# A graph kernel on one core: another order of a pair's products in layer 0, one buffer for x1, banks chosen by hand

## The chip, the core and the metric

The kernel runs on one core of a Trainium2 chip. A core has five engines that run side by side, each through its own list of instructions in order: TensorE (PE in the profile: matmuls; PEld are its weight loads), VectorE (DVE), ScalarE (ACT), GpSimd (POOL) and SyncE (SP), which here issues all the DMAs. An instruction that needs what another engine makes waits on a semaphore, and everything behind it on its own engine waits too. The metric is the time of one execution on the device in microseconds (us), median of several runs.

## The reference

Two layers of a graph network in float32, on 64 graphs of 256 nodes with 256 features, all with one 256 x 256 adjacency:

```python
# layer 0, with G = adj * adj
h = relu(layernorm(x))
h = relu(G @ (h @ W1))          # W1: 256 x 512
h = relu(G @ (h @ W2))          # W2: 512 x 1024
x = x + G @ (h @ W3)            # W3: 1024 x 256
# layer 1, with U the eigenvectors of the normed Laplacian of adj
h = relu(layernorm(x))
h = relu((U.T @ h) @ W1 + b1)   # W1: 256 x 128
x = x + U @ (h @ W2 + b2)       # W2: 128 x 256
```

So the kernel has two jobs that do not depend on each other until layer 1: the eigenvectors of one 256 x 256 matrix (a long chain of small steps, mostly on VectorE), and the matmuls of layer 0 (TensorE).

## The kernel before, in words

**Layer 0** (class `Layers`) goes over 32 pairs of graphs. For pair q the products on TensorE are `first` (G h0, 8 matmuls of 256 columns, copied to y1 by ScalarE), `widened` (times W1, 8 matmuls of 512, relu to s1), `spread_out` (times G, 16 of 256, copied to y2), `third` (times W2, 32 of 512, relu to s2), `fourth` (times W3, 32 of 256, copied to p3) and `last` (G p3, 4 of 512; VectorE adds x and writes x1). Then `norm1` normalizes x1 on ScalarE and GpSimd, `turn_rows` transposes it (8 of 128), `for_layer1` multiplies by layer 1's W1 (8 of 128) and gives hw. x1 and hw go to memory by a DMA, but those of the last two pairs (`KEPT = 2`) stay on the chip.

A float32 matmul of n columns shows as two records in the profile. Every product goes to a PSUM bank of 128 x 512; layer 0 has four, handed out by a pool in turn, and a bank can be taken again when ScalarE or VectorE has read it.

**The order of the work** is written down by `products` (the line of TensorE's work and the ScalarE operations behind it) and `rows` (loads and norms). The order within pair q before is: third(q), turn_rows(q-1), the first half of fourth(q), for_layer1(q-1), first(q+1), the second half of fourth(q), widened and spread_out of q+1, last(q). `rows` begins pair q+1 (load x, norm to h0) and then does norm1 of pair q-1.

**The eigenvectors** (class `Eigen`) share the engines with it. `Pace` is a planner that runs while the program is built: it keeps a clock for each engine with estimated durations, and before each operation of the eigenvector chain it fills the engines with operations from the two streams that fit before that operation is due. It may cut a matmul at a multiple of 128 columns. So the lists of TensorE and ScalarE hold layer 0 and the eigenvector chain interleaved in a fixed order; a wrong estimate becomes a wait. SP has no clock in the plan: a DMA counts as landed 4 us after its data is ready.

At the end of the chain, a flag says whether a rare repair is needed (`mend`): all engines load the flag and branch on it. `pace.go_on(FLAG_US)` puts 3.5 us of TensorE work between the flag's product and the branch. Behind the branch `layer1` runs: a third stream (`layer1_of`) fetches hw and x1 of a pair (`fetch`, two DMAs), multiplies hw by U (`to_vectors`), by U again (`from_vectors`) and by W2 (`finish`), 4 matmuls of 256 each, and writes the output. What is left of layer 0 goes on beside it.

Of the kernel before, what the change touches and what calls it, by code (L numbers as in the profile page):

```python
# [27 lines left out]
N = 256  # L28
P = 128
H = 2  # L30
PAIRS = 32
KEPT = 2
# [48 lines left out]
class Op:  # L81
# [4 lines left out]
    def __init__(self, part, call, args, kwargs):  # L86
# [18 lines left out]
        elif self.engine == "ACT":  # L105
            pointers = any(isinstance(kwargs.get(k), bass.AP) for k in ("scale", "bias"))
            self.busy = 0.13 + n / 1400 + 0.12 * pointers + 0.19 * sums
            self.until = self.busy + 0.12
        elif self.engine == "DVE":
            each = 6.3 if self.name == "reciprocal" else 2.0 if self.name == "tensor_tensor_scan" else 1.0  # L110
            pointers = self.name == "scalar_tensor_tensor" or any(a.shape[1:] == [1] for a in ins[1:])
            self.busy = 0.065 + 0.06 * pointers + each * n / 960 + 0.08 * sums
            self.until = self.busy + 0.125
        elif self.engine == "POOL":
            power = OP.pow in args
            self.busy = 0.2 + (0.14 * n + 0.15 if power else 2 * n / 960)
            self.until = self.busy + 0.1
        else:
            self.busy, self.until = 0.1, 4.0
# [160 lines left out]
class Eigen:  # L280


    def __init__(self, tc, ctx, ap, gt2, pace):
# [5 lines left out]
        self.adj = pool.tile([P, H, N], F32, name="adj")  # L289
        dma(out=self.adj, in_=ap["adj"].rearrange("(h p) n -> p h n", p=P))  # L290
        mats = [pool.tile([P, H, N], F32, name=c) for c in ("ident", "lower", "upinc", "sub")]
        self.mats = mats
        self.ident, self.lower, self.upinc, self.sub = mats
        self.load_matrices(0, 1)
# [9 lines left out]
        self.mp = ctx.enter_context(tc.tile_pool(name="eig_mat", bufs=1))  # L304
# [1465 lines left out]
class Layers:  # L1770


    def __init__(self, tc, ctx, ap, gt2, u, ut):
# [3 lines left out]
        self.kept = ctx.enter_context(tc.tile_pool(name="kept", bufs=KEPT))  # L1777
        dram = ctx.enter_context(tc.tile_pool(name="dram", bufs=1, space=bass.MemoryType.DRAM))
        self.x1, self.hw = {}, {}
        self.x, self.h0, self.y1, self.y2, self.s2, self.p3, self.h1, self.new = ({} for _ in range(8))  # L1780
        self.begun, self.through, self.rows_of = set(), set(), {}
        self.due = False
        self.spilled = {
            q: dram.tile([P, H * 2 * N], F32, name=f"x1_{q}") for q in range(PAIRS - KEPT)
        }
        self.spilled_hw = {
            q: dram.tile([P, H * 2 * P], F32, name=f"hw_{q}") for q in range(PAIRS - KEPT)
        }
# [20 lines left out]
    def load(self, q):  # L1809
        self.x[q] = x = self.io.tile([P, H, 2, N], F32, tag="x", name="x")  # L1810
# [5 lines left out]
    def open(self, ctx):  # L1816

        self.io = ctx.enter_context(self.tc.tile_pool(name="l0_io", bufs=2))
        self.wp = ctx.enter_context(self.tc.tile_pool(name="l0_work", bufs=1))
        self.sp = ctx.enter_context(self.tc.tile_pool(name="l0_stat", bufs=2))  # L1820
        self.ps = ctx.enter_context(self.tc.tile_pool(name="l0_psum", bufs=4, space=PSUM))
# [9 lines left out]
    def bank1(self):  # L1831

        self.turns += 1
        over = PAIRS - 1 in self.through and self.turns % 2
        return (self.ps if over else self.ps1).tile([P, 512], F32, tag="bank", name="bank")
# [4 lines left out]
    def bank(self):  # L1840
        return self.ps.tile([P, 512], F32, tag="bank", name="bank")
# [43 lines left out]
    def products(self):  # L1885
# [3 lines left out]
        for q in range(PAIRS):  # L1889
            more = q + 1 < PAIRS  # L1890
            yield from self.third(q)
            if q > 0:
                yield lambda: q - 1 in self.h1
                yield from self.turn_rows(q - 1)
            yield from self.fourth(q, 0)
            if q > 0:
                yield from self.for_layer1(q - 1)
            if more:
                yield from self.first(q + 1)
            yield from self.fourth(q, 1)  # L1900
            if more:
                yield from self.second(q + 1)
            yield from self.last(q)
        yield lambda: PAIRS - 1 in self.h1 and self.due
        yield from self.turn_rows(PAIRS - 1)
        yield from self.for_layer1(PAIRS - 1)

    def rows(self):

        for q in range(PAIRS + 1):  # L1910
            if q < PAIRS:
                if q > 0:
                    yield lambda: q - 1 in self.begun
                yield from self.begin(q)
            if q > 0:
                yield lambda: q - 1 in self.new
                yield from self.norm1(q - 1)

    def begin(self, q):
        if q not in self.x:  # L1920
            yield from self.load(q)
        x = self.x[q]
# [9 lines left out]
    def first(self, q):  # L1932

        self.y1[q] = self.wp.tile([P, H, 2 * N], F32, tag="y1", name="y1")
# [4 lines left out]
    def first_of(self, q, b):  # L1939
        yield lambda: self.rows_of.get(q, 0) > b  # L1940
        h0, ps = self.h0[q], self.bank()
        for c in range(H):
# [5 lines left out]
            self.y1[q][:, :, b * N : (b + 1) * N], ps.rearrange("p (c n) -> p c n", c=H)  # L1948
        )

    def second(self, q):

        s1, y2 = self.of_second(q)
        for b in range(2):
            yield from self.widened(q, b, s1)
        for b in range(2):
            yield from self.spread_out(b, s1, y2)

    def of_second(self, q):
        s1 = self.wp.tile([P, H, 2, 512], F32, tag="s1", name="s1")  # L1960
        self.y2[q] = y2 = self.wp.tile([P, 512 // P, 2 * N], F32, tag="y2", name="y2")
        return s1, y2

    def widened(self, q, b, s1):
        y1, w1 = self.y1[q], self.w["L0_gnn_W1"]
        for m in range(H):
            ps = self.bank()
            at = b * N + m * P
            yield from self.products_of(ps, [(y1[:, c, at : at + P], w1[:, c, :]) for c in range(2)])
            yield self.nc.scalar.activation(s1[:, m, b, :], ps, AF.Relu)  # L1970

    def spread_out(self, b, s1, y2):
        for c in range(0, 512 // P, 2):
            ps = self.bank()
            for i in range(2):
                at = (c + i) * P
                yield from self.products_of(
                    ps[:, i * N : (i + 1) * N],
                    [(s1[:, h, b, at : at + P], self.gt2[:, h, :]) for h in range(H)],
                )  # L1980
            yield self.nc.scalar.copy(
                y2[:, c : c + 2, b * N : (b + 1) * N], ps.rearrange("p (c n) -> p c n", c=2)
            )

    def first_pair(self):

        self.y1[0] = self.wp.tile([P, H, 2 * N], F32, tag="y1", name="y1")
        s1, y2 = self.of_second(0)
        for b in range(2):
# [3 lines left out]
            yield from self.widened(0, b, s1)  # L1993
            yield from self.spread_out(b, s1, y2)

    def third(self, q):

        nc, w2, y2 = self.nc, self.w["L0_gnn_W2"], self.y2.pop(q)
        self.s2[q] = s2 = self.wp.tile([P, 1024 // P, 2 * N], F32, tag="s2", name="s2")
        for j in range(1024 // P):  # L2000
            ps = self.bank()
            yield from self.products_of(ps, [(w2[:, c, j * P : (j + 1) * P], y2[:, c, :]) for c in range(4)])
            yield nc.scalar.activation(s2[:, j, :], ps, AF.Relu)

    def fourth(self, q, m):

        nc, w3, s2 = self.nc, self.w["L0_gnn_W3"], self.s2[q]
        if q not in self.p3:
            self.p3[q] = self.wp.tile([P, H, 2 * N], F32, tag="p3", name="p3")
        ps = self.bank()  # L2010
        for b in range(2):
            at = b * N + m * P
            yield from self.products_of(
                ps[:, b * N : (b + 1) * N],
                [(s2[:, j, at : at + P], w3[:, j, :]) for j in range(1024 // P)],
            )
        yield nc.scalar.copy(self.p3[q][:, m, :], ps)

    def last(self, q):

        nc, x, p3 = self.nc, self.x.pop(q), self.p3.pop(q)
        x1 = self.kept.tile([P, H, 2, N], F32, tag="x1", name="x1")
        for m in range(H):
            ps = self.bank()
            yield from self.products_of(ps, [(self.gt2[:, h, m * P : (m + 1) * P], p3[:, h, :]) for h in range(H)])
            yield nc.vector.tensor_tensor(flat(x1)[:, m, :], flat(x)[:, m, :], ps, OP.add)
        if q in self.spilled:
            yield nc.sync.dma_start(out=self.spilled[q], in_=x1.rearrange("p h b f -> p (h b f)"))
        else:
            self.x1[q] = x1  # L2030
        self.new[q] = x1

    def norm1(self, q):

        x1 = self.new[q]
        scale, shift = (self.sp.tile([P, H * 2], F32, tag=c, name=c) for c in ("scale1", "shift1"))
        yield from self.norm(x1, scale, shift)
        h1 = self.normed("h1")
        yield from self.relu_norm(x1, scale, shift, h1)
        self.h1[q] = h1  # L2040

    def turn_rows(self, q):

        nc, h1 = self.nc, self.h1[q]
# [11 lines left out]
    def for_layer1(self, q):  # L2056

        nc, ht = self.nc, self.h1.pop(q).rearrange("p c b f -> p c (b f)")
        hw = self.kept.tile([P, H, 2, P], F32, tag="hw", name="hw")
# [12 lines left out]
        if q in self.spilled:  # L2072
            yield nc.sync.dma_start(out=self.spilled_hw[q], in_=hw.rearrange("p h b k -> p (h b k)"))
        else:
            self.hw[q] = hw
# [9 lines left out]
    def fetch(self, q):  # L2085
        if q in self.spilled:
            hw = self.io1.tile([P, H, 2, P], F32, tag="hw", name="hw1")
            x1 = self.io1.tile([P, H, 2, N], F32, tag="x", name="x1")
            yield self.nc.sync.dma_start(out=hw.rearrange("p h b k -> p (h b k)"), in_=self.spilled_hw[q])
            yield self.nc.sync.dma_start(out=x1.rearrange("p h b f -> p (h b f)"), in_=self.spilled[q])  # L2090
            self.fetched[q] = x1, hw

    def to_vectors(self, q):

        nc = self.nc
        x1, hw = self.fetched.pop(q) if q in self.spilled else (self.x1[q], self.hw[q])
# [139 lines left out]
```

## Time and profile before

| what | value |
|---|---|
| median of 3 runs | 2414.57 us (2413.95 to 2415.11) |
| the profiled execution | 2414.28 us, of which 2412.2 us from the first to the last instruction (span) |
| TensorE busy | 2373.4 us, 98% of the span |
| VectorE, ScalarE, GpSimd busy | 2003.3, 970.3, 612.0 us |
| DMA | 89.95 MB, 16 engines busy 10.8% of the span |
| granted TensorE clock | 1.0 throughout |
| TensorE, idle in the first 60 us / 60 to 2130 us / 2130 to 2300 us / behind that | 13.4 / 19.0 / 2.4 / 4.8 us |

The last row is worked out from the busy time of TensorE in stretches of the span. A busy TensorE does not mean that nothing waits: the table of waits, by engine, names who ended each idle time. In the timeline, a row is a run of like instructions: start, time, engine, operation, tiles, count, and in brackets the idle time ahead of it with what ended it.

The chain ends (its last product, psC<-bad) at 2151.74 us; layer 1 begins at 2161.89 us. Up to there layer 0 fills TensorE; about two pairs of it are left then.

### The profile page before, as it was taken

Reading aid. Unit: us, or ns where it says so; the run is one execution under the profiler, and the core shown is the slowest. Engines: PE = TensorE matmul, PEld = TensorE weight load, DVE = VectorE, ACT = ScalarE, POOL = GpSimd, SP = SyncE. Lnnn points to the kernel's source line nnn. Section 1 sums busy time; section 2 is a strip of 40 time slices with the busy share of each in tenths; the row PEclk is TensorE's granted clock in tenths of the full one; section 3 lists DMA queues with packets and bytes.
Section 4 is the critical chain, followed back from the end, with each engine's and each line's share of the span. In section 5 each row is a group of like instructions: output and inputs, shape, how many; then the busy total and the mean of one; then the engine's idle time right before and its main releaser. Section 6 shows DMA issues by size and latency. Waiting matters only on the chain. (4 is left out here: it accounts for less than half of the span.)

```text
span 2412.2 us, 37157 instructions
## 1 busy us (share of the span) xinstructions
PE 2373.4 (98%) x9226; PEld 1582.0 (66%) x9226; DVE 2003.3 (83%) x12064; ACT 970.3 (40%) x2602; POOL 612.0 (25%) x1853
## 2 busy tenths in 40 slices
PE   7999999999999999999999999999999999999999
PEld 4666666666666666666666666665666667666888
DVE  7999999999999999999998999998978778830233
ACT  4334444433444443344444244444443343443322
POOL 3444444444443221222221000000000110121243
PEclk9999999999999999999999999999999999999999
DMA  3000000000000000000000000000000000020475
GB/s 114 18 23 5 22 23 18 23 23 5 23 23 19 23 23 22 15 14 23 23 19 30 10 23 23 23 23 18 23 27 22 23 23 5 22 93 31 140 252 179
DMA packets 59390, 89.95 MB, mean 37 GB/s; under 512 B 5792, under 2 KB 42784, under 8 KB 59168
## 3 DMA queue, kind: packets, MB, share of 16 engines
q1 hardware_dynamic: 59168, 87.52, 10.8%
q8 instruction: 74, 1.21, 0.2%
q14 instruction: 148, 1.21, 0.2%
HBM read 47.13 MB, written 40.37 MB: 36 GB/s over the span
## 5 line engine op out<-in xcount | busy, mean ns | idle before, releaser
L208 PE MATMUL bank<-y,L_gnn_W 128*128 128x512 f32 (+3 forms) x2188 | 906.7, 565 | 0.3 <-DVE x L208 0.3
L208 PEld LDWEIGHTS bank<-y,L_gnn_W 128*128 128x128 f32 x2188 | 403.2, 190 | 434.5 <-issue 413.3
L208 PE MATMUL bank<-L_gnn_W,s 128*128 128x256 f32 (+1 forms) x2100 | 463.2, 374 | 1.7 <-PEq L1766 1.0
L208 PEld LDWEIGHTS bank<-L_gnn_W,s 128*128 128x128 f32 x2100 | 387.7, 190 | 50.9 <-issue 1.9
L208 ACT ACTIVATE s<-bank 128x512 f32<-128x512 f32 x384 | 225.1, 588 | 230.6 <-PE bank L208 229.5
L208 PE MATMUL bank<-gt,s 128*128 128x256 f32 (+1 forms) x1036 | 231.8, 377 | 0.8 <-ACT s L208 0.7
L208 PE MATMUL bank<-L_gnn_W,y 128*128 128x512 f32 (+2 forms) x534 | 229.9, 575 | 1.1 <-ACT y L208 1.1
L208 PEld LDWEIGHTS bank<-gt,s 128*128 128x128 f32 x1036 | 193.5, 190 | 38.5 <-issue 11.5
L208 POOL COPY m<-xr 128x1 f32<-128x1 f32 x254 | 56.1, 221 | 467.3 <-DVE xr L208 467.2
L208 ACT COPY y<-bank 128x512 f32<-128x512 f32 x192 | 111.7, 583 | 153.9 <-PE bank L208 153.3
L208 ACT ACTIVATE h<-x,shift,scale 128x256 f32<-128x256 f32 x256 | 136.7, 590 | 71.0 <-POOL shift L208 63.7
L208 PEld LDWEIGHTS bank<-L_gnn_W,y 128*128 128x128 f32 x534 | 99.0, 190 | 99.0 <-issue 94.0
L208 ACT ACTIVATE junk<-xr 128x254 f32<-128x254 f32 (+63 forms) x127 | 45.9, 361 | 256.6 <-DVE xr L208 256.2
L208 DVE SCALAR_TENSOR_TENSOR A<-xr,wc,A 128x255 f32<-128x255 f32 (+63 forms) x381 | 140.2, 370 | 0.0
L208 DVE SCALAR_TENSOR_TENSOR A<-wr,q,A 128x255 f32<-128x255 f32 (+63 forms) x381 | 138.7, 366 | 0.0
L208 ACT ACTIVATE junk<-x 128x256 f32<-128x256 f32 x256 | 105.7, 413 | 81.2 <-DVE x L208 70.1
L208 ACT ACTIVATE junk<-x,nm 128x256 f32<-128x256 f32 x256 | 129.2, 505 | 6.1
L208 PE MATMUL bank<-gt,h 128*128 128x256 f32 (+1 forms) x516 | 119.3, 380 | 0.1
L208 PE MATMUL bank<-p,gt 128*128 128x512 f32 (+2 forms) x266 | 117.9, 576 | 0.0
L208 DVE SCALAR_TENSOR_TENSOR r<-A,xr 128x255 f32<-128x255 f32 (+63 forms) x381 | 117.8, 309 | 0.1
L208 ACT ACTIVATE s<-nn,guard 128x1 f32<-128x1 f32 x127 | 37.3, 294 | 194.7 <-DVE nn L208 171.8
L208 DVE TENSOR_TENSOR out<-xb,bank 128x512 f32<-128x512 f32 x64 | 43.9, 688 | 83.4 <-PE bank L208 77.9
(605 smaller groups left out, 4222.3 us busy)
## 6 DMA issues: line engine op xcount, KB each, us to landing
x<-x SPq DMA_DIRECT2D x60, 512.0 KB, 3.4
x<-in_x_dram SPq DMA_DIRECT2D x64, 256.0 KB, 3.7
out_dram<-out SPq DMA_DIRECT2D x64, 256.0 KB, 2.2
hw<-hw SPq DMA_DIRECT2D x60, 256.0 KB, 2.7
L_gnn_W<-in_L_gnn_W_dram SPq DMA_DIRECT2D x1, 2048.0 KB, 10.3
L_gnn_W<-in_L_gnn_W_dram SPq DMA_DIRECT2D x1, 1024.0 KB, 12.8
L_gnn_W<-in_L_gnn_W_dram SPq DMA_DIRECT2D x1, 512.0 KB, 5.7
mask<-in_c_blk_dram SPq DMA_DIRECT2D x2, 256.0 KB, 3.1
```

Source lines behind the costliest of these rows:

```text
L208: return op.call(*op.args, **op.kwargs)
```

## The change: what it does

The order within pair q becomes: third(q), in which last(q-1) is done (half of it after the first, half after the second of the eight blocks of W2), first(q+1), widened(q+1), turn_rows(q-1), and then spread_out of q+1 in four blocks with fourth(q) between them: block, a quarter of fourth, for_layer1(q-1), the load of x into x1, block, a quarter, block, a quarter, block, a quarter. So first(q+1) has widened(q+1) right behind it, where half of fourth(q) stood before.

x1 is one tile for all pairs: x of pair q is loaded a second time, straight into it, VectorE adds G p3 in place, the norm and the transposes write over it. x, the tile that is normed to h0, has one buffer in place of two, and the norm of pair q+2 is done during pair q. Layer 0's four banks are picked by `bank` and can be held (`fourth` holds two of them through its four quarters). s2 is laid out in another order, so that each relu of 128 x 512 behind W2 becomes two of 128 x 256. No pair is kept on the chip: the last two are written out and fetched too. adj lies in the tile m4 of the eigenvector part in place of a tile of its own.

The diff also brings a way to multiply by W2 with seven products in place of eight (`spread_by_seven`, `third_by_seven`, `fold_weights`, `seventh`, `rectify`, `add`). It would begin at pair `SEVEN_FROM = 99`; there are 32 pairs, so it never runs, and it is left out here, as are the planner's cost of a GpSimd DMA, which has no use then, and renamings.

```diff
-KEPT = 2
+SEVEN_FROM = 99
...
-        self.adj = pool.tile([P, H, N], F32, name="adj")
...
+        self.adj = self.mat("m4")
...
+        self.s2 = pool.tile([P, 2, 4, 2, N], F32, name="s2")
+        self.p3 = pool.tile([P, H, 2 * N], F32, name="p3")
+        self.x1 = pool.tile([P, H, 2, N], F32, name="x1")
...
-        self.io = ctx.enter_context(self.tc.tile_pool(name="l0_io", bufs=2))
+        self.io = ctx.enter_context(self.tc.tile_pool(name="l0_io", bufs=1))
...
-        self.ps = ctx.enter_context(self.tc.tile_pool(name="l0_psum", bufs=4, space=PSUM))
+        self.ps = ctx.enter_context(self.tc.tile_pool(name="l0_psum", bufs=1, space=PSUM))
+        self.banks, self.held = list(range(4)), {}
...
-    def bank(self):
-        return self.ps.tile([P, 512], F32, tag="bank", name="bank")
+    def bank(self, held=False):
+
+        i = next(i for i in self.banks if i not in self.held.values())
+        self.banks.append(self.banks.pop(self.banks.index(i)))
+        ps = self.ps.tile([P, 512], F32, tag=f"bank{i}", name="bank")
+        if held:
+            self.held[ps.tensor.name] = i
+        return ps
+
+    def free(self, ps):
+        i = self.held.pop(ps.tensor.name)
+        self.banks.append(self.banks.pop(self.banks.index(i)))
...
-            yield from self.third(q)
+            last = self.last(q - 1) if q > 0 else iter(())
+            for part in self.third_by_seven() if seven else self.third():
+                if part is None:
+                    yield from next(last, ())
+                else:
+                    yield part
+            if more:
+                yield from self.first(q + 1)
+                for b in range(2):
+                    yield from self.widened(b)
...
             if q > 0:
                 yield lambda: q - 1 in self.h1
-                yield from self.turn_rows(q - 1)
-            yield from self.fourth(q, 0)
+                yield from self.turn_rows()
+            yield from next(forms, ())
...
+            products = self.fourth()
+            yield from next(products)
             if q > 0:
                 yield from self.for_layer1(q - 1)
-            if more:
-                yield from self.first(q + 1)
-            yield from self.fourth(q, 1)
-            if more:
-                yield from self.second(q + 1)
-            yield from self.last(q)
+            for i in range(2):
+                yield self.nc.sync.dma_start(out=self.x1[:, i], in_=self.view(self.ap["x"], q)[:, i])
+            for part in products:
+                yield from next(forms, ())
+                yield from part
...
+        yield from self.begin(0)
+        for q in range(PAIRS):
+            for p in [1, 2] if q == 0 else [q + 2]:
+                if p < PAIRS:
+                    yield lambda: p - 1 in self.begun
+                    yield from self.begin(p)
+            yield lambda: q in self.new
+            yield from self.norm1(q)
...
-            yield nc.scalar.activation(s2[:, j, :], ps, AF.Relu)
+            for b, out in enumerate(self.s2_of(j)):
+                yield nc.scalar.activation(out, ps[:, b * N : (b + 1) * N], AF.Relu)
+            yield None
...
+    def fourth(self):
+
+
+        order = [0, 1, 4, 5, 2, 3, 6, 7]
+        banks = [self.bank(held=True) for _ in range(H)]
+
+        def part(m, b, at):
+            for i in at:
+                yield self.nc.tensor.matmul(
+                    banks[m][:, b * N : (b + 1) * N],
+                    lhsT=self.s2_of(order[i])[b][:, m * P : (m + 1) * P],
+                    rhs=self.w["L0_gnn_W3"][:, order[i], :],
+                    start=i == 0,
+                    stop=i == 7,
+                )
...
+        yield first_half(range(4))
+        yield first_half(range(4, 8))
+        for m in range(H):
+            yield second_half(m)
...
+            yield nc.vector.tensor_tensor(flat(x1)[:, m, :], flat(x1)[:, m, :], ps, OP.add)
+            if m == H - 1:
+                yield nc.sync.dma_start(out=self.spilled[q], in_=x1.rearrange("p h b f -> p (h b f)"))
+                self.new.add(q)
...
+        yield from self.relu_norm(self.x1, scale, shift, self.x1)
```

In the changed program TensorE has 5131 matmuls and transposes (5144 before, by other cuts of the same columns), ScalarE 256 instructions more (the halved relus), SP 72 DMAs more: 64 of 256 KB for x1, and 2 x 4 for the two pairs that were kept, of hw and x1, out and in.

## The prediction

> **What bounds the kernel now.** First the page: busy shares and clock.
>
> ```profile
> PE 2373.4 (98%) x9226; PEld 1582.0 (66%) x9226; DVE 2003.3 (83%) x12064; ACT 970.3 (40%) x2602; POOL 612.0 (25%) x1853
> ...
> PEclk9999999999999999999999999999999999999999
> ```
>
> TensorE is busy 2373.4 of 2412.2 us at full clock, so only its 38.8 idle us can go, and any new wait on it is paid in full. Busy could still hide slow matmuls; the timeline of a late pair says no:
>
> ```profile
> 2094.01 7.07 PE L208 MATMUL bank<-L_gnn_W,s 128*128 128x256 f32 x32
> 2100.92 7.03 PE L208 MATMUL bank<-L_gnn_W,y 128*128 128x512 f32 x16
> ```
>
> A record takes 0.22 us for 256 columns and 0.44 for 512, in step with the columns; a matmul has two records, so 0.43 and 0.87 us, 1.69 ns per column. 128 columns cost 0.12 per record (16 in 1.95 us). The time follows the columns, which the change leaves as they are; other cuts cost about 0.01 us each.
>
> Then the waits of TensorE:
>
> ```profile
> PE psB L208 <- DVE z L208: 6.0, 8, 1.2
> PE psC L208 <- DVE c L208: 5.5, 1, 5.5
> PE psB L208 <- DMA ident<-in_c_mats_dram: 4.9, 1, 4.9
> PE psB L208 <- DVE xr L208: 2.7, 5, 1.5
> ...
> PE bank L208 <- ACT s L208: 1.4, 3, 0.6
> ...
> PE bank L208 <- PEq L1766: 1.0, 1, 1.0
> ```
>
> The psA to psD waits are the eigenvector chain's: 10.4 us at the start, 18.6 later. The bank waits are layer 0's own: 3.5 us, and 1.0 at the branch. So layer 0 has almost nothing to gain from a better order; the question is what the new order lays open. The end, some 4 us of add and output DMA behind the last matmul, stays.
>
> **Parts that cost nothing, and what hides them.** Matmuls: same columns, 13 fewer pieces, under 0.3 us. Relus halved: ScalarE's 128x256 copy out of PSUM takes 0.379 us (z<-psC) against 0.588 for 128x512, so 0.17 more, 256 times, 44 us on an engine busy 970; behind W2 the next use of a bank is at least 6.9 us of matmuls away, and the two halves need 0.31 + 0.76. Moving G p3 into W2: its ScalarE copies lie 4.3 us ahead where 0.9 is needed; without that cover it would be 0.9 x 31. VectorE's add keeps 8.65 us until its bank is wanted, as before. x1 in one buffer: its load stands behind for_layer1 on SP's queue, 19 us of TensorE work ahead of the add; x loads land in 3.7 us and the DMA engines are 6% busy in this stretch. x in one buffer: the load waits for the four h0 relus, but a pair lasts 67 us and its norm begins in the next. On SP the x1 load, the hw write and the x1 write stand in the order in which their producers end, so none holds another up for long. The in-place norm waits for the x1 write (3.4 us); ScalarE's eight sums ahead of it take over 5. The last two pairs' round trip, 1.5 MB each way: its reads come three steps (15.6 us) ahead of use, at 63% DMA load.
>
> [...]
>
> **The branch, a cost.** The end of the eigenvector chain, and the first fetch:
>
> ```profile
> 2153.70 1.89 PE L208 MATMUL bank<-L_gnn_W,s 128*128 128x256 f32 x8
> ...
> 2156.63 5.42 PE L208 MATMUL bank<-L_gnn_W,s 128*128 128x256 f32 x24 [1.04 <-PEq L1766]
> ...
> 2157.14 0.34 SPq L208 DMA_DIRECT2D hw<-hw  x1
> ...
> 2161.89 0.59 PE L208 MATMUL bank<-hw,u 128*128 128x256 f32 x2
> ```
> ```profile
> DMA to landing us min/median/max: 2.9/2.9/2.9
> ```
>
> TensorE comes out of the branch at 2156.63; hw of pair 0 is issued at 2157.14 and lands at 2160.04. Twelve matmuls of W3 (5.2 us) happened to stand in between. In the built order of the changed program the first instruction behind the branch is that layer 1 matmul, with nothing ahead of it: the plan keeps no clock for SP, and takes the fetch as long landed. Everything on TensorE queues behind it. The wait: 2160.04 + 0.1 - 2156.63 = 3.5 us; ahead of the branch stand four 512-column matmuls (3.5 us) where 3.7 us stood, 0.15 more. **+3.65 us.** Bounds: 2.8 if the DMA lands like the fastest kind on the page (2.2), 5.9 if like the median fetch of this stretch (5.2).
>
> [...]
>
> **Thin covers, a cost that no row shows.** Before, half of W3 (7 us) stood between first(q+1) and widened(q+1). Now W1 follows G h0 at once: the copy of the first half of y1 has only the second half, 1.73 us, plus a piece of the eigenvector chain in half of the pairs (median 2.6). What it needs is seen in the first pair, where nothing stood between:
>
> ```profile
> 27.49 1.03 PE L208 MATMUL bank<-gt,h 128*128 128x256 f32 x4
> 29.20 1.98 PE L208 MATMUL bank<-L_gnn_W,y 128*128 128x512 f32 x4 [0.68 <-ACT y L208]
> ```
>
> The last of the four records begins its last 0.22 at 28.14, ends near 28.36, and W1 starts at 29.20: 0.84 us with ScalarE free. So 0.9 us of slack, 31 times, against an instruction of the eigenvector chain in between (0.29 to 0.55 us, in about five pairs, or as long as VectorE is late). The second place is behind widened: the first block of spread_out and the first of W3 take banks that widened's relus give back 2.77 us of matmuls later (5.2 before). The relu needs 0.31 + 0.59, but the sums of a norm are planned between these relus:
>
> ```profile
> L208 ACT ACTIVATE junk<-x,nm 128x256 f32<-128x256 f32 x256 | 129.2, 505 | 6.1
> ...
> L208 ACT ACTIVATION_READ_ACCUMULATOR junk<-x,nm 128x1 f32 x256 | 47.9, 187 | 0.0
> ```
>
> One takes 0.505 + 0.187 = 0.69 us, or 0.60 (the first kind, 0.413 + 0.187). Eight of them, 5.2 us, four relus, 2.4, and two to three eigenvector instructions, about 1, make 8.6 us of ScalarE in the 8.0 us of widened and the transposes. So ScalarE comes out of it 0.6 us behind or more, of 1.9 us slack; where two sums stand ahead of the last relu it is gone. I take 2 us in all (a quarter of 31 pairs, 0.25 us each); bounds 0 (slack holds everywhere) and 12 (0.4 in each pair). A gain is excluded here: these waits were 3.5 us in all, mostly in the first pair, which stays.
>
> **The eigenvector chain.** By columns its last product stands 12.5 us earlier. That frees nothing, for TensorE has layer 0 to do until layer 1 takes over; it leaves that much more of it behind the branch. Its 18.6 us of later waits are due times in the plan missed by VectorE by up to 1.5 us. The new order draws them anew: 0, between -9 (psB's 8.7 vanish) and +5.
>
> **Sum.** 2414.28 (the profiled execution: span 2412.2 and 2.1 around it; 0.3 below the median of the runs) + 3.65 + 2 + 0 = 2419.9; with the 0.3, about **2420**.
>
> **Rivals.**
> 1. Branch only, the thin covers hold: 2414.6 + 3.65 = 2418.2, not slower by the bound below. For it: ScalarE is busy 40%, slack is positive nearly everywhere. Against it: the load of 8.6 in 8.0 us.
> 2. ScalarE becomes the bound behind widened: 0.3 to 0.5 us lost in every pair, 31 x 0.4 = 12, with the branch 2430. It decides where VectorE's results, for which ScalarE waits in its queue (256 us of idle <-DVE xr before), come later than planned.
> 3. Faster: the chain's psB waits (8.7 us, 13 times) vanish as the new blocks push its transposes later: 2414.6 + 3.65 - 8.7 = 2409.5. It decides only if the thin covers cost nothing too. Against it: the planner and its due times are unchanged.
> 4. The change does not do what it says: sevenfold products never run (99 pairs), so nothing is saved; that is in the forecast.
>
> **Chances.** About 0.2%, 4.8 us, is what a measurement of this kernel can tell from no change: 2409.7 to 2419.4. Forecast (2419.4 to 2425) 0.38, slower. Rival 1 (2412 to 2419.4) 0.38, same, and 0.02 between it and rival 3, same. Rival 2 (above 2425) 0.15, slower. Rival 3 0.07, faster. So 0.07, 0.40, 0.53. The forecast and rival 1 hold most: 2412 to 2425. For 8 in 10 with half of rival 2: 2411 to 2429.
>
> **What would show it.** Right: a wait of 3 to 5 us of TensorE on hw's DMA at the branch; waits on ACT y and ACT s spread over the pairs, 1 to 6 us in all; TensorE busy 2373 +- 2. Wrong: the fetch landed before TensorE comes out; waits on DMA in the pairs (x1 or x late, single buffers); layer 1 waiting for pairs 30 and 31; psB waits far from 8.7.

## The result, and the profile after

The changed kernel takes **2436.16 us** (median of 4 runs, 2431.29 to 2438.55), the kernel before 2414.7 (2413.95 to 2415.11): a ratio of 1.0087, 95% interval 1.0069 to 1.0104. The profiled execution took 2438.55 us, its span is 2436.8: 24.6 us more than before. The four runs differ in the mean granted clock of TensorE too: 0.997 at 2431.29 us, 0.996 at 2435.12, 0.995 at 2437.2 and 2438.55; the kernel before has 1.0 in each. So the profiled execution is the longest of the four, and what follows is worked out for it. The page says in which form the time came:

```profile
PE 2386.0 (98%) x9200; PEld 1583.0 (65%) x9200; DVE 2000.0 (82%) x12064; ACT 975.0 (40%) x2858; POOL 604.3 (25%) x1853
...
PEclk9999999999999999999999999999999999999999
```

TensorE is busy 12.6 us longer (2373.4 before) for the same columns, and idle 12.0 us longer (50.8 us for 38.8). The clock row of 40 slices shows nothing; a slice is 61 us wide. The waits of TensorE, whole run (us in all, times, longest):

```profile
PE psC L208 <- DVE c L208: 6.6, 1, 6.6
PE bank L208 <- ACT y L208: 5.6, 3, 4.5
PE psB L208 <- DVE z L208: 4.9, 9, 1.1
PE bank L208 <- DMA hw<-hw: 4.9, 1, 4.9
PE bank L208 <- ACT x L208: 4.6, 3, 2.7
...
PE bank L208 <- DVE x L208: 2.5, 1, 2.5
...
PE bank L208 <- ACT s L208: 1.8, 3, 1.1
```

Against before: hw at the branch +3.9 (4.9 for the 1.0 behind PEq, TensorE's own sequencer, which takes the branch), y +4.5, x by ScalarE +4.6, x by VectorE +2.2, s +0.4, start of the chain +0.7, its later waits -3.4 (15.2 for 18.6). So a few long waits, not many short ones. One of them in the timeline:

```profile
1540.06 3.62 PE L208 MATMUL bank<-gt,h 128*128 128x256 f32 x16
1543.51 3.60 PE L208 MATMUL bank<-L_gnn_W,y 128*128 128x512 f32 x8
1550.88 0.22 ACT L208 ACTIVATE q<-q 128x15 f32<-128x15 f32 x1 [8.24 <-DVE q L208]
1551.01 0.57 ACT L208 COPY y<-bank 128x512 f32<-128x512 f32 x1
1551.63 6.49 PE L208 MATMUL bank<-L_gnn_W,y 128*128 128x512 f32 x8 [4.52 <-ACT y L208]
```

The second half of G h0 ends at 1543.5. Its copy to y stands in ScalarE's list behind `q`, a small instruction of the eigenvector chain that waits 8.24 us for VectorE; W1 has only its own first half to do meanwhile. And the same eight records take 3.60 us ahead of the wait, 6.49 behind it. The granted clock, in windows laid around it (PE busy, PEld, DVE, ACT, POOL, then PEclk, DMA share and GB/s) and around the branch:

```profile
1540.00:1547.00 7.00, 7.00 (x25) 4.37 (x23) 6.51 (x52) 2.18 (x8) 0.23 (x1) 1.00 0.00 1
1551.00:1557.00 6.00, 5.37 (x7) 2.28 (x8) 5.65 (x44) 5.90 (x22) 0.23 (x1) 0.50 0.00 0
...
2162.50:2168.00 5.50, 5.50 (x9) 2.95 (x10) 0.00 (x0) 0.00 (x0) 3.62 (x3) 0.50 0.96 339
2168.50:2172.00 3.50, 3.50 (x12) 1.94 (x11) 0.69 (x1) 1.08 (x3) 3.50 (x4) 1.00 0.97 383
```

Behind each of five places the clock is 0.50: 6.8 us behind the y wait, 3.4 behind VectorE's x (1866.5), 3.4 behind ScalarE's x (1973.7), 6.8 at the branch, 3.4 in layer 1 (2291, two waits of 1.2 and 0.7 close together). That is 23.9 us at half clock, of which 2.1 lie within the two longest waits themselves; half of the other 21.8, 10.9 us, is lost, most of the 12.6 of added busy time. The two x waits have the same pattern on other engines:

```profile
1865.49 0.35 DVE L208 SCALAR_TENSOR_TENSOR m<-mask,ncur,m 128x128 f32<-128x128 f32 x1
1865.76 0.68 DVE L208 TENSOR_TENSOR x<-x,bank 128x512 f32<-128x512 f32 x1
1866.49 11.19 PE L208 MATMUL bank<-forms,L_gnn_W 128*128 128x512 f32 x22 [2.50 <-DVE x L208]
...
1970.20 0.70 POOL L208 TENSOR_TENSOR rdq<-rdq,half 128x2 f32<-128x2 f32 x1 [6.61 <-DVE rdq L208]
...
1972.58 0.60 ACT L208 ACTIVATE h<-x,shift,scale 128x256 f32<-128x256 f32 x1 [6.26 <-POOL shift L208]
1973.70 3.66 PE L208 MATMUL bank<-L_gnn_W,x 128*128 128x128 f32 x16 [2.71 <-ACT x L208]
```

The add of G p3 is queued behind the chain on VectorE, and W2 wants its bank. The copy of the turned x1 is behind a norm's `h` on ScalarE, that behind `shift` on GpSimd, that behind `rdq`, for which VectorE comes late.

**Is VectorE later than before?** No. ScalarE's waits for this `q`, before and after:

```profile
ACT q L208 <- DVE q L208: 73.6, 24, 8.5
```
```profile
ACT q L208 <- DVE q L208: 73.8, 24, 8.2
```

Before, the longest of them fell here:

```profile
1608.88 7.07 PE L208 MATMUL bank<-L_gnn_W,s 128*128 128x256 f32 x32
...
1617.57 3.62 PE L208 MATMUL bank<-gt,h 128*128 128x256 f32 x16
1618.88 0.22 ACT L208 ACTIVATE q<-q 128x15 f32<-128x15 f32 x1 [8.55 <-DVE q L208]
1619.00 0.57 ACT L208 COPY p<-bank 128x512 f32<-128x512 f32 x1
...
1620.08 0.59 ACT L208 COPY y<-bank 128x512 f32<-128x512 f32 x1
1621.03 7.07 PE L208 MATMUL bank<-L_gnn_W,s 128*128 128x256 f32 x32
1621.23 0.59 ACT L208 COPY y<-bank 128x512 f32<-128x512 f32 x1 [0.57 <-PE bank L208]
1627.93 4.46 PE L208 MATMUL bank<-L_gnn_W,y 128*128 128x512 f32 x10
```

ScalarE waited as long as in the changed kernel, with copies queued behind it, but TensorE had W3 to do until 1627.9, 6 us past the second copy of y.

Call the cover of a copy the work that TensorE has between what is copied and the first matmul that needs it.

**Theory.** The branch costs its wait and the clock behind it. The rest: some instructions of the chain stand in the lists of ScalarE, GpSimd and VectorE up to 8 us too early, as before, and in the new list what is queued behind three of them is wanted at once. **Rivals:** the load on ScalarE (halved relus, norms a pair ahead) makes the copies late; or the loss lies in the thin cover of y alone.

### The profile page after: what moved, and what is told of

Its sections match the earlier page's. It is cut to its first block, busy times and chain, and to the rows that moved or that the text cites. A ratio compares the mean times of both kernels' runs of the same rounds, so it can differ in the third digit from the quotient of the medians.

```text
span 2436.8 us, 37593 instructions
## 1 busy us (share of the span) xinstructions
PE 2386.0 (98%) x9200; PEld 1583.0 (65%) x9200; DVE 2000.0 (82%) x12064; ACT 975.0 (40%) x2858; POOL 604.3 (25%) x1853
## 5 line engine op out<-in xcount | busy, mean ns | idle before, releaser
L208 PE MATMUL bank<-forms,L_gnn_W 128*128 128x512 f32 (+2 forms) x2178 | 920.8, 569 | 2.5 <-DVE x L208 2.5
L208 PEld LDWEIGHTS bank<-forms,L_gnn_W 128*128 128x128 f32 x2178 | 402.0, 191 | 425.6 <-issue 402.5
L208 PE MATMUL bank<-L_gnn_W,s 128*128 128x256 f32 x2080 | 470.9, 376 | 0.0
L208 ACT ACTIVATE s<-bank 128x256 f32<-128x256 f32 (+1 forms) x640 | 242.2, 418 | 339.0 <-PE bank L208 337.7
L208 PE MATMUL bank<-gt,s 128*128 128x256 f32 (+1 forms) x1042 | 246.5, 376 | 1.9 <-ACT s L208 1.8
L208 PE MATMUL bank<-L_gnn_W,y 128*128 128x512 f32 (+3 forms) x538 | 233.7, 578 | 5.7 <-ACT y L208 5.6
L208 PEld LDWEIGHTS bank<-L_gnn_W,y 128*128 128x128 f32 x538 | 100.1, 192 | 104.4 <-issue 89.0
L208 ACT COPY forms<-bank 128x512 f32<-128x512 f32 x128 | 74.2, 580 | 101.9 <-PE bank L208 101.8
L208 PEld LDWEIGHTS bank<-gt,h 128*128 128x128 f32 x516 | 97.3, 192 | 23.4 <-issue 10.5
## 6 DMA issues: line engine op xcount, KB each, us to landing
L_gnn_W<-in_L_gnn_W_dram SPq DMA_DIRECT2D x1, 2048.0 KB, 10.6
```

The source lines that it names most:

```text
L208: return op.call(*op.args, **op.kwargs)
```

## The experiments

Each time stands beside that of the kernel before on the same chip (2413.7 to 2415.6).

**The branch.** `e1`: the plan may not start a DMA of layer 1 ahead of the branch, so it knows when hw lands.

```diff
+        elif engine == "SP":
+            start = max(start, self.sp_from)
...
+            pace.sp_from = pace.clock["PE"] + 0.5    # in layer1, at the branch
```

> The changed kernel, with the plan told that the fetches begin only behind the branch, so that seven W2 matmuls (6 us) stand between the branch and layer 1's first matmul. Theory (each long wait of TensorE is paid twice, as the wait and as a halved granted clock for 3.4 or 6.8 us behind it): the wait on hw (4.9 us, 1.0 stays) and its 6.8 us of half clock (2.9 us) go, 2436.2 - 6.8 = about 2429; the clock stays at 1.0 there. Rival A (the lower clock has nothing to do with the waits): only the wait goes, 2432. Rival B (the added time is spread load, ScalarE's 256 instructions and 18 MB of DMA): 2436.

2426.2 us, ratio 1.0043 (1.0029 to 1.0057): 10.6 us over the kernel before instead of 21.5, so some 11 came back, more than the theory's 6.8. The waits now have

```profile
PE bank L211 <- PEq L1769: 1.3, 1, 1.3
```

in place of hw's 4.9. With it went the two small x waits of layer 1 and their half clock (by the profile 3.6 us of wait and 3.0 of clock at the branch, 1.9 and 1.7 in layer 1: 10.2); the y wait (4.8), VectorE's x (2.5) and ScalarE's x (2.7) stayed, each with its half clock. `e2`: the kernel before, with layer 1's first matmul put first behind the branch.

```diff
+            while True:
+                op, stream.op = stream.head(), None
+                pace.issue(op)
+                if op.engine == "PE":
+                    break
```

> The kernel before, with layer 1's first matmul put ahead of the twelve W3 matmuls behind the branch, and nothing else moved. Theory: a wait of about 3.5 us, and 3.4 to 6.8 us of half clock behind it (1.7 to 3.4 us lost): 2414.7 + 5.2 to 6.9 = 2420 to 2421.6. Rival A: the wait alone, 2418.2. Rival B: the branch is not where the time went, 2414.7.

2420.54, ratio 1.0021 (1.0012 to 1.0030): +4.9 by this wait alone. The interval, 2.9 to 7.2 us, does not tell the theory (5.2 to 6.9) from rival A (3.5, the wait alone); the profile does: its span is 6.4 us longer, 4.1 of wait and 2.2 of busy time, and the clock is 0.50 behind the wait:

```profile
2160.27 1.19 PE L208 MATMUL bank<-hw,u 128*128 128x256 f32 x2 [5.08 <-DMA hw<-hw]
```
```profile
2159.00:2165.50 6.50, 5.23 (x12) 4.21 (x13) 0.00 (x0) 0.00 (x0) 2.70 (x3) 0.50 0.86 297
```

`e8`: the same with six W3 matmuls ahead of it.

> The kernel before, with layer 1's first matmul behind six of the twelve W3 matmuls that follow the branch: TensorE comes out of the branch, works 2.6 us and then waits for hw some 2.5 us less than where nothing stood ahead (5.1 us with the branch in it). Theory (a wait past some length halves the clock for one window of 3.4 us, whatever its length): 1.0 at the branch and a wait of about 1.0 to 1.5 us; if that is still too long, 1.7 us lost behind it, 2414.7 + 1.2 + 1.7 = 2417.6; if not, 2416. Rival A: 2416 with the clock at 1.0.

2415.22, ratio 1.0004: waits of 1.16 and 0.71 us, and

```profile
2158.00:2166.00 8.00, 7.29 (x42) 6.35 (x41) 0.03 (x1) 0.91 (x2) 3.20 (x3) 1.00 0.87 288
```

The theory's "one window of 3.4 us, whatever its length" doesn't fit the trace of `e2`: there the clock is 0.50 for 6.8 us. Here the short waits cost their length; the long one of `e2` cost half as much again through the clock (2.2 on 4.1).

**The cover.** `e3`: half of W3 again between G h0 and W1 in the changed kernel.

```diff
             if more:
                 yield from self.first(q + 1)
-                for b in range(2):
-                    yield from self.widened(b)
...
+            yield from next(products)
+            if more:
+                for b in range(2):
+                    yield from self.widened(b)
+                forms = self.spread_in_turn()
```

> The changed kernel, with half of W3 back between G h0 and W1: third with last, first(q+1), turn_rows, two quarters of fourth, widened(q+1), then two blocks of spread_out ahead of each of the last two quarters. So the copy of y1 has 7 us and more in place of 1.7, and the x copies stand in another place. Theory: the waits on ACT y (4.5 us) and ACT x (2.7) go with the half clock behind them (2.8 and 1.7): 2436.2 - 11.7 = 2424 to 2425 if the branch wait and the wait on VectorE's add stay and no new one comes. Rival A: the waits alone, 2429. Rival B: 2436.

2436.92: no gain, the expectation fell. The y waits went (1.6 us), but s waits came, 11.1 us in 11, and the longest has the same root:

```profile
2112.75 2.07 ACT L208 ACTIVATE h<-x,shift,scale 128x256 f32<-128x256 f32 x4 [8.83 <-POOL shift L208]
2115.36 4.86 PE L208 MATMUL bank<-L_gnn_W,y 128*128 128x512 f32 x6 [5.17 <-ACT s L208]
```

So the thin cover behind G h0 by itself isn't it. Two things moved in this run, though: the list was dealt anew, and hw's wait at the branch fell to 1.4 us with it.

**The load.** `e5`: a relu behind W2 is one instruction of 128x512 again.

> The changed kernel, with the relus behind W2 whole again (128 x 512, 256 ScalarE instructions fewer). Rival B (the added time is ScalarE's added load): the long waits go or shrink with it, 2415 to 2425. Theory (a few layer 0 operations stand behind an instruction of the eigenvector chain that comes late): the built list is dealt anew, so which waits there are may change, but there will be two to five long ones again, the one on hw among them, each with 3.4 or 6.8 us of half clock: 2428 to 2440.

2424.4, ratio 1.0041, in the rival's range and outside the theory's; but hw's wait at the branch had also gone to 0.8 us, because the list was dealt anew, so this run alone decides nothing. `e9` does the same where the fetch and the lateness are dealt with (`e7`, below):

> The changed kernel with three things undone or set at once: the plan knows of layer 1's first fetch, the eigenvector chain's operations are planned later (factors 1.25 and 1.13), and a relu behind W2 is one instruction of 128x512 again. Without the third it took 2414.4 us. Theory (long waits come from late instructions ahead in ScalarE's and VectorE's queues, at any load): 2412 to 2417, no change that counts; ScalarE busy some 20 us less than 975 as with the whole relus alone. Rival (ScalarE's load of 975 us is what makes its copies late, and the whole relus alone gained 12 us by that): the gain adds to the other two, 2404 to 2408.

2419.64, 5 us slower than `e7`, with ScalarE busy 17 us less. The load rival falls: it forecast a gain. The theory's number (2412 to 2417) falls too: TensorE is idle 5.9 us more, in several places (psB behind z 6.9 for 4.7, one wait for y2 2.8 for 1.6), with nothing but these relus and the list changed. `e11` and `e11k`: the norm of pair q+2 behind that of x1 of pair q, in the changed kernel and in `e7`.

```diff
-            for p in [1, 2] if q == 0 else [q + 2]:
-                if p < PAIRS:
-                    yield lambda: p - 1 in self.begun
-                    yield from self.begin(p)
             yield lambda: q in self.new
             yield from self.norm1(q)
+            if q + 2 < PAIRS:
+                yield lambda: q + 1 in self.begun
+                yield from self.begin(q + 2)
```

> The changed kernel with one part undone: the norm of pair q+2 stands behind that of x1 of pair q again, not ahead of it. Theory (the sums and scalars of a norm in the stretch of widened are only one of the things queued ahead of a copy; the long waits come where an eigenvector instruction on ScalarE or GpSimd waits for a late VectorE): the branch's 4.9 us stay, long waits stay in number (2 to 5 in the pairs) but at other places, 2425 to 2440. Rival (the norm a pair ahead is what loads ScalarE and GpSimd at the wrong place): the waits on ACT x and the GpSimd shift go, only the branch stays, 2418 to 2422.

> The norm of pair q+2 behind that of x1 of pair q, in the version that has the first fetch in the plan and the later plan (2414.4 us without this edit). Theory: no change that counts, 2412 to 2418, for no long wait is left there but one on VectorE's x of 3 us. Rival (the norms a pair ahead still cost short waits): 2408 to 2412, faster than both kernels.

2446.27 and 2430.45, 10 and 16 us slower than their bases; all four expectations miss. The cause is in the table of waits (of `e11`):

```profile
PE bank L208 <- ACT h L208: 18.7, 8, 4.6
```

In the new order G h0 comes right behind W2, and without the norm a pair ahead h0 comes late, eight times. So the norms a pair ahead are what the new order needs, not what costs.

**The lateness.** `e4`: in the changed kernel the chain's operations are planned with longer durations, in its blocks and in its levels, so ScalarE and TensorE meet them later. `e6`: the same in the kernel before. `e7`: `e4` with `e1`.

```diff
-    SLOWER, IN_BLOCKS = 1.06, 1.13
+    SLOWER, IN_BLOCKS, IN_LEVELS = 1.06, 1.25, 1.13
...
-        self.pace.slower, self.pace.lead = self.pace.SLOWER, 0.0
+        self.pace.slower, self.pace.lead = self.pace.IN_LEVELS, 0.0
```

> The changed kernel, with the plan's durations of the eigenvector chain longer (factor 1.25 in place of 1.13 in the leaves, 1.13 in place of 1.06 in the levels), so that layer 0's ScalarE, GpSimd and VectorE operations are not put behind chain instructions that come later than planned. Theory (the three waits between 1500 and 2000 us are layer 0 operations queued behind a late instruction of the chain): they go, 9.7 us, with 6.2 us lost to the half clock: 2436.2 - 16 = 2420, the branch wait left. Rival C (the order itself leaves too little cover, whatever the plan thinks): ACT y and ACT x waits stay, 2430 to 2436. The chain's end moves 70 us later, still ahead of the end of layer 0.

> The kernel before, with the longer plan of the experiment on later due times (1.25 in the leaves, 1.13 in the levels). Theory: before has no long wait to lose there, so it gains at most the short ones (3.6 us between 1500 and 2000 us) and its chain still ends ahead of layer 0: 2411 to 2416. If it gets slower by over 5 us, the longer plan has a price of its own, which the changed kernel pays too.

> The changed kernel with both: the plan knows when the fetches begin, and the longer plan. Theory: 2419.9 less the wait on hw of 2.5 us (1.0 stays) and its 1.7 us of half clock: 2416.5, the same as before within 0.2%; what stays is one wait of 3.2 us on VectorE's add with 1.7 us behind it. Rival B: no lower than 2419.

2419.85 (ratio 1.0019), 2414.72 (1.0005, 0.9996 to 1.0014) and 2414.41 (1.0001, 0.9992 to 1.0010). The long y wait and ScalarE's x are gone with the late `q` (its longest wait is now 2.2 us), and `e7` has given back the whole loss. It still has a wait of 3.1 us on VectorE's x, at 1786.7, with 3.4 us of half clock behind it, so a later plan does not remove every long wait. `e10` goes the other way: the kernel before, planned earlier (1.05 and 1.0).

> The kernel before, with the eigenvector chain's operations planned earlier (factors 1.05 and 1.0 in place of 1.13 and 1.06), so that VectorE comes later than planned by more. Theory (the old order has wide covers between its products, 7 us of W3 between G h0 and W1, so a late eigenvector instruction in ScalarE's queue costs little, and the lateness costs only the chain's own waits): layer 0's waits on ACT and DVE stay under 6 us in all, psB to psD waits grow from 18.6 later us to 25 to 40, 2418 to 2430. Rival (the old order is as frail and was only well timed): ACT y, ACT s and ACT x waits of over 2 us with the clock at half behind them as in the changed kernel, and 2430 or more.

2439.64: the rival was right in the time, the old order is as frail, and in part in the reason. ScalarE's waits for `q` grew to 133.1 us, TensorE's for s to

```profile
PE bank L208 <- ACT s L208: 11.0, 8, 3.4
```

with five stretches of 3.4 us at half clock: two behind waits for s (3.4 and 1.8 us), three behind waits of the eigenvector chain itself (2.7, 2.3 and 1.8). Is it a trend with the factor, or is each list a draw? Six more factors, four on the changed kernel with the fetch known, two on the kernel before:

> The changed kernel with the first fetch in the plan, and the chain's operations planned earlier than in it: factors 1.10 and 1.04 (it has 1.13 and 1.06, 2426.2 us; at 1.25 and 1.13 it takes 2414.4). Theory (the plan's lateness sets the loss): more long waits, 2428 to 2440. Rival (each list is a draw and the factor means little): anywhere between 2412 and 2428.

> The same at 1.16 and 1.075. Theory: a loss between those at 1.13 and 1.25, 2417 to 2424. Rival (a draw): no order with its neighbours.

> The same at 1.21 and 1.11. Theory: close to the value at 1.25, 2413 to 2419. Rival (a draw): no order with its neighbours, 2420 or more is as likely as not.

> The same at 1.32 and 1.17. Theory: the ScalarE waits on DVE q are gone already at 1.25, so nothing is left to win but the 3 us wait on VectorE's x and its half clock: 2409 to 2416. Rival (a draw): 2412 to 2425, with other long waits.

> The kernel before with the chain planned a little earlier: factors 1.10 and 1.04 (it has 1.13 and 1.06). Theory (each order has a stretch of factors in which its list has no long wait, and the new order's lies at later plans than the old one's): some loss already, 2417 to 2432. Rival (the old order has no such edge near 1.13; the loss at 1.05 is that one list's): 2412 to 2417.

> The kernel before with the chain planned later: factors 1.20 and 1.095, between its own and those that took 2414.7 us. Theory: no change that counts, 2412 to 2417. Rival (each list is a draw): 2418 or more, or under 2411, as likely as not.

| factor in blocks | old order, us | ScalarE for `q` | new order, fetch known, us | ScalarE for `q` |
|---|---|---|---|---|
| 1.05 | 2439.6 | 133.1 | | |
| 1.10 | 2429.3 | 100.1 | 2422.8 | 79.4 |
| 1.13 | 2414.7 (before) | 73.6 | 2426.2 | 75.7 |
| 1.16 | | | 2414.7 | 58.2 |
| 1.20, 1.21 | 2421.3 | 12.7 | **2410.5** | 12.1 |
| 1.25 | 2414.7 | 7.6 | 2414.4 | 9.9 |
| 1.32 | | | 2429.1 | 3.0 |

Both: the lateness of VectorE falls steadily with the factor, in both orders alike, and where it is large the time tends to be long. But the time doesn't follow it point by point. At 1.13 the new order is slower than at 1.10. At 1.16 it has one wait of 5.6 us (for y2) with 6.8 us of half clock, and still takes the time of the kernel before: by its profile the rest of TensorE's idle time is about 8 us shorter than there. The old order lost at 1.20, where it has a wait of 4.0 us on VectorE's x with 3.4 us of half clock, and where its list too has the layer 1 matmul first behind the branch:

```profile
2201.04 1.19 PE L208 MATMUL bank<-hw,u 128*128 128x256 f32 x2 [5.82 <-DMA hw<-hw]
```

At 1.32 the plan is too late: the chain ends at 2248.5 instead of 2153.6 us in the changed kernel, TensorE runs out of layer 0 and waits 5.7 us for the chain and 7.9 for hw. At 1.21 no wait behind the first 60 us is over 1.5 us, the clock never drops, TensorE is busy 2373.8 us, and between 1500 and 2000 us, where the changed kernel lost most (its row first, then that of 1.21), it has hardly any idle time:

```profile
1500.00:2000.00 500.00, 487.07 (x1731) 309.25 (x1730) 412.71 (x2490) 195.11 (x572) 40.18 (x82) 0.99 0.08 27
```
```profile
1500.00:2000.00 500.00, 499.56 (x1786) 316.92 (x1785) 416.81 (x2527) 205.33 (x598) 42.74 (x83) 1.00 0.09 28
```

That version takes 2410.53 us against 2413.81 of the kernel before, ratio 0.9983 (0.9974 to 0.9993): the fastest of all, by 0.17%. It is the best of six factors tried for the new order, against five for the old, so part of this may be the luck of the choice.

## Why the prediction failed, step by step

- **Direction** and the **branch mechanism** were right: TensorE waits there on hw's DMA, 3.9 us more than before for 3.65 forecast (whose lower bound, 2.8, leaves out the 0.15 that the forecast and the upper bound have in them). The term still was mis-sized: the step priced a wait by its length. `e2` shows 4.9 us for such a wait alone, and in the changed kernel its removal was worth 10 to 11, since two x waits in the list behind it, with a half clock of their own, went with it.
- **The missing term: the clock.** "any new wait on it is paid in full" was the step that failed; a long one is paid in full and then in part again: behind the 4.5 us of the y wait 2.8 more went at a clock of 0.50. 10.9 of the 24.6 us are half clock. The forecast of TensorE busy 2373 +- 2 is refuted (2386.0); without the half clock it would be 2375.1, at its edge, so the columns were counted about rightly. The stretches here last 3.4 or 6.8 us, and not only the waits of 4.5 and 4.9 us brought them on: those of 2.5 and 2.7 us did too. This bears on every term of the sum that is a wait.
- **Thin covers**: the term was 2 us, spread as 0.25 us over a quarter of the pairs. It measured 4.9: 4.5 (y) and 0.4 (s). The two x waits in the pairs, which the sum put at nothing, came to 4.9 more (ScalarE's 2.7, VectorE's 2.2 more than before). That is 9.8 us, not spread but nearly all in three places. The slack was compared with the duration of the instruction queued ahead (0.29 to 0.55 us) and "as long as VectorE is late" was named and not priced, though the table of ScalarE's waits had it: 24 waits, longest 8.5 us. One wait of 8.2 us used up the cover of y and 4.5 us beyond it.
- **"VectorE's add keeps 8.65 us"** failed in one pair: the add stood behind the chain in VectorE's own queue (2.5 us).
- **Rival 2** named the condition rightly (VectorE later than planned), but priced it as ScalarE's load, a little in each pair; `e9` refutes the load.
- **Held**: the halved relus (no cost of their own seen; they added 17 to 18 us to ScalarE's busy time, by `e5` and `e9`, where the prediction had 44), single x and x1 (no wait for their DMAs in the pairs), the last two pairs' round trip (no wait behind 2300 us), the chain's later waits (-3.4 us, inside -9 to +5).
- **The range** took a wait for a small, even cost. The runs show what the list alone makes of one order: 2414.7 to 2439.6 us of the old one, which stood at the best of the points tried, and 2410.5 to 2429.1 of the new one with its fetch known.

**What stays open.** Which of the lists has a long wait can't be read from the order: neither the halved relus nor the cover, undone alone, accounts for the 12 us beside the branch. The timelines show instructions of the chain ahead in a queue before each of the three long waits, and a later plan removed those on y and on ScalarE's x and left one on VectorE's x; each such run dealt the whole list anew, so no run moved one of these instructions alone. That 1.13 fits the old list and not the new one because of where those instructions happened to stand is argued, not shown. The single buffers were not undone.

## What to carry to other kernels

Where lists are dealt out by a planner, compare a cover with the longest wait of what may be queued ahead of it (here 8 us), not with that instruction's duration, and price a long wait on TensorE with the half clock behind it (here in all 24 cases from 2.95 us on, and in 14 of 25 between 1.78 and 2.81). A change of order leaves the point at which the planner's factors were good; try some factors with the new order before judging it: the same order took 2410.5 and 2429 us.

## What the runs showed of the hardware

The granted clock after a wait of TensorE, from all 20 traces of this study, the first 60 us left out (the clock records of a trace begin only 15 to 19 us into it, and the two waits of over 4 us in those 60 us end by 13.0):

- 20 waits of 1.4 to 1.75 us brought no drop. Shorter ones did twice, two close together each time: 1.2 and 0.7 us in layer 1 of the changed kernel, 1.3 and 1.0 us in the new order at 1.10.
- Of 25 waits between 1.78 and 2.81 us 14 brought one stretch of 3.4 us at 0.50, 11 none.
- All 24 of 2.95 us and more did, the 12 up to 4.1 us with 3.4 us (8) or 6.8 us (4), the 12 from 4.5 to 7.9 us always with 6.8.

So a wait between 1.8 and 2.8 us cost 0 or 1.7 us on top of itself (half of a stretch of 3.4); one of over 4.5 us had 6.8 us at 0.50, up to 3.4 us lost, less what of them lies within the wait (2.8 and 3.0 us were lost at the two long ones of the changed kernel).

Between 1.8 and 2.8 us the length of a wait does not tell which of the two it is: one of 1.89 us in `e3` and one of 2.71 in the changed kernel had 3.4 us at 0.50 behind them, while behind 2.54 us in `e16` and 2.81 in `e9` the clock stayed at 1.00. What decides there was not shown.
